# Masks on two row halves, and attention directly ahead of the second step of scores in TensorE's order

## The chip, the cores and the metric

The kernel runs on one core of one Trainium2 chip. The metric is the device time of one execution in microseconds. A core has TensorE (matrix products, PE in the profile, its weight loads PEld), VectorE (DVE), ScalarE (ACT), GpSimd (POOL) and the DMA queue that SyncE issues (SP). Each engine works through its own instructions in a fixed order and waits on the others by semaphores.

## The reference

The input is `x` of 8 sequences x 512 tokens x 128 features. A layer norm without gain gives `xn`, and the result is the sum of three parts.

```python
xn = _layernorm(x)
x = x + attn(xn, ...) + ffn(xn, ...)
```

`attn` is one causal attention with 16 heads of 8 features and relative positions. `ffn` is, in spite of its name, a stack of six layers. Each layer has a local attention and a feed-forward part, both with a residual:

```python
for i in range(DEPTH):                                  # 6
    x = attn_layer(shift_tokens(x), ...) + x            # 16 heads of 64, windows of 32
    x = ffn_layer(shift_tokens(x), ...) + x             # layer norm, 128 -> 2*341, gelu gate, -> 128
```

In `attn_layer`, queries and keys are normalised to unit length per head and rotated. Every window of 32 queries sees its own 32 keys and the 32 keys before it, with this mask:

```python
mask = (it < jb) | (it > jb + w) | (jb == -1)
sim = jnp.where(mask, -jnp.finfo(sim.dtype).max, sim)
attn = jax.nn.softmax(sim, -1)
```

The mask of a query depends on its place in its window only, and, for the first window of a sequence, on the fact that there are no earlier keys.

## The kernel before

The single causal attention (`rel_attention`) runs first, some 500 us. The six local layers (`local_layers`, `steps_of_layers`) fill the rest. Their work is cut into tiles of 128 tokens: 6 layers x 8 sequences x 4 tiles are 192 tiles. The loop over tiles is a hand-written software pipeline. In iteration `n` TensorE works on several tiles at once, and the order of its instructions is exactly the order of the program (`tc.manual_schedule` for TensorE alone). A planner lays out the queues of the other engines at build time by its own estimates of when operands are ready. The order of the steps of one iteration is a string of `ORDERS`, one for each tile position in a sequence: row `n % 4`, called rows 0 to 3 here. The steps are:

- `p0` to `p3` project queries (0, 1) and keys (2, 3) of tile `n + 2`. Each is three products into one PSUM buffer (L641 to L643); VectorE rotates (L771, L772), ScalarE squares (L773), GpSimd adds (L776), VectorE sums the squares (L779 for one part, L781 for the other).
- `r` makes the inverse norms of tile `n + 2` on VectorE (a chain of small operations, L791, L70 to L81), and GpSimd multiplies queries and keys by them (L795). It holds nothing for TensorE.
- `q0 q1 k0 k1` turn queries and keys of tile `n + 1` (L814), and ScalarE copies them out (L817).
- `s0`, `s1` are the two steps of scores of tile `n`. Each fills two PSUM banks. A matmul with an identity first writes the mask into each bank (L836), then 64 matmuls of a 64 x 32 part of the array add the scores (L848). VectorE takes the maxima (L857), and ScalarE makes the exponentials with their sums, eight pairs of instructions (L861). After `s1` the reciprocal of the sums is taken (L873), GpSimd multiplies (L874), and VectorE transposes (`pT`, L876). There are only two such banks (`PSB = (2, 6)`), so the masks of one step wait for the exponentials of the step before.
- `v0` to `v3` make values of tile `n`, already multiplied by the output weights: three products, a copy by ScalarE (L890), and four DMAs on SP's queue (`vw`, L892).
- `a0`, `a1` are attention for tile `n - 1` (`attend`): 64 short matmuls of probabilities and values (L910; 56 for the first tile of a sequence) into one PSUM buffer, then a copy by ScalarE (`ys`, L921).
- `+` adds the result of tile `n - 2` to the state `xt` (a turn at L928, VectorE at L931). After the last tile of a sequence it also starts that sequence's feed-forward part. Each `f` runs one step of that: a split, the mean (L945), the variance (L953), the scaling (L978), three gates and their gelu (L1001), three values, and the output (`f_ps`, L1023), which VectorE adds (L1035).
- `w1`, `w2` make the next layer's value weights on L727 at the first tile of a layer only. Those matmuls work on two row halves: features 0 to 63 into one bank, 64 to 127 into another.

All products but the scores use six PSUM buffers of one pool (`ps_x`) in turn, the inverse norms' scratch (`root_tile`) too.

Of the kernel before, what the change touches and what calls it, by code (L numbers as in the profile page):

```python
# [13 lines left out]
BF16 = mybir.dt.bfloat16  # L14
# [6 lines left out]
P = 128  # L21
# [20 lines left out]
H, D = 16, 64  # L42
# [3 lines left out]


ORDERS = (
    "p0 p1 v0 f s0 w2 + p2 f p3 q0 f f q1 s1 w2 k0 v1 w1 a0 r a1 w1 k1 v2 v3",
    "p0 s0 w2 p1 p2 v0 q0 f p3 f + f q1 s1 w2 k0 v1 w1 a0 r a1 w1 k1 v2 v3 f",  # L50
    "p0 p1 s0 w2 v0 v1 f p2 q0 q1 p3 s1 w2 k0 w1 + a0 r a1 w1 k1 v2 v3",
    "p0 p1 s0 w2 v0 f p2 q0 + q1 p3 v1 s1 w2 k0 w1 a0 r a1 w1 k1 v2 v3",
)
PSB = (2, 6)
VAR = {'Z': '', 'N': '', 'C': '0', 'D': 0, 'hl': 'P', 'xl': 'P', 'fl': 'P', 'v': 'AAAA', 'q': 'AA', 'k': 'AA', 'pr': 'P', 'R5': 0, 'lo2': 'V'}
# [527 lines left out]
def local_layers(tc, i, ident, ident_b, xt, out, spare):  # L583


    with ExitStack() as ctx:
        yield from steps_of_layers(ctx, tc, i, ident, ident_b, xt, out, spare)


def steps_of_layers(ctx, tc, i, ident, ident_b, xt, out, spare):  # L590
    nc = tc.nc

    def pool(name, bufs, **kw):
        return ctx.enter_context(tc.tile_pool(name=name, bufs=bufs, reuse_waits="tile", **kw))
# [13 lines left out]
    def eng(c):  # L608
        return nc.gpsimd if c == "P" else nc.vector
# [4 lines left out]
    def in_turn(step):  # L614


        ins = step.ins
        if "any" in last:
            tc.add_manual_dep(
                ins,  # L620
                last["any"].name,
                mybir.DependencyInfo(mybir.DependencyClass.NoSync, mybir.DependencyReason.DATA),
                reason="one table at a time",
            )
        last["any"] = ins
# [193 lines left out]
    def scores(n, g):  # L819

        t = tiles[n][2]
        if g == 0:
            probs[n] = {
                "pr": p2.tile([P, 2, 2, NW, 2 * W], F32, name="pr"),
                "mx": p2.tile([P, 2, 2, NW], F32, name="mx"),
                "sm": p2.tile([P, 2 * 2 * NW], F32, name="sm"),
            }  # L830
        pr, mx, sm = (probs[n][k] for k in ("pr", "mx", "sm"))
        qT, kT = turned[n]["q"], turned[n]["k"]
        mask = masks[:, 0 if t == 0 else 1].rearrange("p w k -> p (w k)")
        banks = [ps_sc.tile([P, NW, 2 * W], F32, name="sc_ps") for _ in range(2)]
        for ps in banks:
            nc.tensor.matmul(  # L836
                ps.rearrange("p w k -> p (w k)"),
                lhsT=ident_b,
                rhs=mask,
                start=True,  # L840
                stop=False,
                skip_group_check=True,
            )
        for w in range(NW):
            for j in range(4):
                for p, ps in enumerate(banks):
                    r = slice(D * p, D * p + D)
                    nc.tensor.matmul(  # L848
                        ps[32 * j : 32 * j + 32, w, :],
                        lhsT=qT[r, 4 * g + j, W * w : W * w + W],  # L850
                        rhs=kT[r, 4 * g + j, W * w : W * w + 2 * W],
                        start=False,
                        stop=w == NW - 1,
                        skip_group_check=True,
                    )
        for p, ps in enumerate(banks):
            nc.vector.tensor_reduce(mx[:, p, g], ps, AX.X, ALU.max, negate=True)  # L857
            for w in range(NW):
                m = (2 * p + g) * NW + w
                in_turn(  # L860
                    nc.scalar.activation(  # L861
                        pr[:, p, g, w, :],
                        ps[:, w, :],
                        AF.Exp,
                        bias=mx[:, p, g, w : w + 1],
                        accum_out=sm[:, m : m + 1],
                    ),
                )
        if g == 0:
            return  # L870
        del turned[n]
        flat = pr.rearrange("p a g w k -> p (a g w) k")
        nc.vector.reciprocal(sm, sm)  # L873
        eng(VAR["pr"]).tensor_mul(flat, flat, sm.unsqueeze(2).to_broadcast([P, 16, 2 * W]))  # L874
        pT = p2.tile([P, 2, 2, NW, 2, W], F32, name="pT")
        nc.vector.transpose(  # L876
            pT.rearrange("p a g w b q -> p (a g w b q)"), pr.rearrange("p a g w k -> p (a g w k)")
        )
        probs[n] = pT
# [200 lines left out]
    cp = pool("b_const", 1)  # L1080
    p1 = pool("b_p1", 1)
    p2 = pool("b_p2", 2)
    p3 = pool("b_p3", 3)
# [13 lines left out]
    nc.vector.memset(keys[:, :, 0:W], 0.0)  # L1097
    ones = cp.tile([P, P], F32R, name="ones")
    nc.vector.memset(ones.bitcast(F32), 1.0)
    mean_w = cp.tile([P, 1], F32, name="mean_w")  # L1100
    nc.vector.memset(mean_w, 1.0 / E)

    with tc.manual_schedule(engines={nc.tensor.engine}):
        for n in range(-1, len(tiles) + 2):
# [10 lines left out]
            for step in ORDERS[n % NT].split():  # L1115
# [8 lines left out]
                elif kind == "r" and more:  # L1124
                    normalise(n + 2)
                elif kind == "q" and have(n + 1):
                    turn_q(n + 1, k)
                elif kind == "k" and have(n + 1):
                    turn_k(n + 1, k)
                elif kind == "s" and have(n):  # L1130
                    scores(n, k)
                elif kind == "v" and have(n):
                    values(n, k)
                elif kind == "a" and have(n - 1):
                    attend(n - 1, k)
                elif kind == "+" and have(n - 2):
                    add(n - 2)
                    l, b, t = tiles[n - 2]
                    if t == NT - 1:
                        if l not in weights:  # L1140
                            weights[l] = load(l)
                        feeding = feed_forward(l, b, weights[l])
                elif kind == "f":
                    next(feeding, None)
                elif kind == "w":

                    if have(n + k) and tiles[n + k][1:] == (0, 0):
                        next(making, None)
# [95 lines left out]
```

## Time and profile before

| | |
|---|---|
| three runs | 3472.5, 3478.84 (median), 3479.6 us |
| profiled execution | 3475.25 us, span 3473.3 us, granted TensorE clock 0.988 |
| busy share of the span | PE 94%, PEld 69%, DVE 88%, ACT 80%, POOL 80% |
| mask matmuls (L836) | 768, busy 173.5 us, 278 ns each with their pipeline |
| a steady group of four tiles (2089.1 to 2148.5 us) | 59.4 us: PE 57.50 busy, DVE 54.16, ACT 51.13, POOL 51.02 |

Line numbers with an L are lines of the kernel before. In a list of waits, a line names the engine and tile that waited, whom it waited for, the total in us, how often, and the longest. In a chain or timeline, a line begins with its start and its length in us from the start of the span. An instruction's form such as 64*32 gives the rows and columns of the array that it uses. Matmuls are pipelined, so the distance between the starts of two matmuls tells what one costs, not its length.

### The profile page before, as it was taken

Reading aid. Unit: us, or ns where it says so; the run is one execution under the profiler, and the core shown is the slowest. Engines: PE = TensorE matmul, PEld = TensorE weight load, DVE = VectorE, ACT = ScalarE, POOL = GpSimd, SP = SyncE. Lnnn points to the kernel's source line nnn. Section 1 sums busy time; section 2 is a strip of 40 time slices with the busy share of each in tenths; the row PEclk is TensorE's granted clock in tenths of the full one; section 3 lists DMA queues with packets and bytes.
Section 4 is the critical chain, followed back from the end, with each engine's and each line's share of the span. In section 5 each row is a group of like instructions: output and inputs, shape, how many; then the busy total and the mean of one; then the engine's idle time right before and its main releaser. Section 6 shows DMA issues by size and latency. Waiting matters only on the chain.

```text
span 3473.3 us, 130619 instructions
## 1 busy us (share of the span) xinstructions
PE 3253.4 (94%) x50176; PEld 2393.9 (69%) x50176; DVE 3039.7 (88%) x7474; ACT 2791.2 (80%) x9818; POOL 2768.1 (80%) x2130
## 2 busy tenths in 40 slices
PE   6999989999999999899999999998999999999997
PEld 4666657777677777677777677776777776777775
DVE  8788748999899999989998898999989899898994
ACT  3776668888788888788888788888888888888884
POOL 5666668888888888888888788888888888788883
PEclk9999989999999999999999999999999999999998
DMA  1111123232333322333233332323333233233332
GB/s 43 33 33 42 30 64 80 72 74 72 86 82 78 75 72 73 96 77 76 70 75 75 86 84 73 74 72 91 76 77 76 72 74 94 73 83 76 83 76 59
DMA packets 221058, 249.93 MB, mean 72 GB/s; under 512 B 73238, under 2 KB 115604, under 8 KB 220436
## 3 DMA queue, kind: packets, MB, share of 16 engines
q1 hardware_dynamic: 220148, 241.18, 28.2%
q8 instruction: 398, 6.52, 0.8%
q14 instruction: 224, 1.84, 0.2%
q10 hardware_dynamic: 288, 0.39, 0.0%
HBM read 26.92 MB, written 4.19 MB: 9 GB/s over the span
## 4 chain that ended last, share of the span: by engine, by line
PE 44%; DVE 29%; ACT 17%; issue 3%; POOL 3%; DMA 3%; SPq 1%; ACTq 0%; POOLq 0%; DVEq 0%
ACT pr L861 7%; PE y_ps L910 7%; PE qkT_ps L814 6%; DVE q L771 5%; DVE rot L772 5%; PE sc_ps L848 4%; PE f_ps L1023 3%; PE v_ps L641 2%; ACT h L1001 2%; PE v_ps L642 2%; ACT sq L773 2%; DVE pT L876 2%; PE a_o_ps L467 2%; PE v_ps L643 2%; DVE mx L857 2%
## 5 line engine op out<-in xcount | busy, mean ns | idle before, releaser
L861 ACT ACTIVATE pr<-sc_ps,mx 128x64 f32<-128x64 f32 x3072 | 923.1, 347 | 114.8 <-DVE mx L857 110.4
L776 POOL TENSOR_TENSOR q<-q,rot 128x1024 f32<-128x1024 f32 x384 | 934.2, 2433 | 93.1 <-DVE rot L772 58.1
L795 POOL TENSOR_TENSOR q<-q,rn 128x1024 f32<-128x1024 f32 x384 | 725.5, 1910 | 2.1 <-DVE rn L81 1.6
L861 ACT ACTIVATION_READ_ACCUMULATOR pr<-sc_ps,mx 128x1 f32 x3072 | 717.7, 240 | 0.0
L773 ACT ACTIVATE sq<-qk_ps 128x512 f32<-128x512 f32 x768 | 469.8, 632 | 251.7 <-DVE rot L772 158.4
L874 POOL TENSOR_TENSOR pr<-pr,sm 128x1024 f32<-128x1024 f32 x192 | 365.7, 1905 | 340.4 <-DVE rn L81 213.1
L771 DVE TENSOR_TENSOR q<-qk_ps,wrot 128x512 f32<-128x512 f32 x768 | 523.9, 682 | 43.3 <-PE qk_ps L643 38.3
L772 DVE TENSOR_TENSOR rot<-qk_ps,wrot 128x512 f32<-128x512 f32 x768 | 521.4, 679 | 0.0
L890 ACT COPY v<-v_ps 128x512 f32<-128x512 f32 x768 | 469.8, 660 | 52.6 <-PE v_ps L643 24.5
L814 PE MATMUL qkT_ps<-ident,q 128*128 128x128 f32 x3072 | 479.9, 282 | 23.4 <-POOL q L795 14.7
L814 PEld LDWEIGHTS qkT_ps<-ident,q 128*128 128x128 f32 x3072 | 340.2, 141 | 143.8 <-POOL q L795 54.9
L848 PEld LDWEIGHTS sc_ps<-kT,qT 64*32 64x32 f32 x24576 | 272.6, 106 | 180.4 <-issue 178.9
L910 PE MATMUL y_ps<-vw,pT 128*32 128x128 f32 x11904 | 382.5, 275 | 3.6 <-DMA vw<-v 3.4
L910 PEld LDWEIGHTS y_ps<-vw,pT 128*32 128x32 f32 x11904 | 328.1, 110 | 58.1 <-issue 27.3
L641 PE MATMUL qk_ps<-wqk_hi,xs_hi 128*128 128x512 f32 x768 | 349.0, 454 | 19.4 <-ACT ys L921 15.8
L641 PE MATMUL v_ps<-wvo_hi,xs_hi 128*128 128x512 f32 x768 | 339.6, 442 | 11.5 <-ACT ys L921 6.4
L848 PE MATMUL sc_ps<-kT,qT 64*32 64x64 f32 x24576 | 335.6, 226 | 0.7 <-ACT kT L817 0.7
L643 PE MATMUL qk_ps<-wqk_hi,xs_lo 128*128 128x512 f32 x768 | 305.7, 398 | 0.0
L643 PE MATMUL v_ps<-wvo_hi,xs_lo 128*128 128x512 f32 x768 | 304.4, 396 | 0.0
L642 PE MATMUL qk_ps<-wqk_lo,xs_hi 128*128 128x512 f32 x768 | 304.2, 396 | 0.0
L642 PE MATMUL v_ps<-wvo_lo,xs_hi 128*128 128x512 f32 x768 | 303.1, 395 | 0.0
L857 DVE TENSOR_REDUCE mx<-sc_ps 128x4 f32<-128x256 f32 x768 | 282.8, 408 | 11.1 <-PE sc_ps L848 9.5
(201 smaller groups left out, 7198.8 us busy)
## 6 DMA issues: line engine op xcount, KB each, us to landing
vw<-v SPq DMA_DIRECT2D x3072, 64.0 KB
a_qz<-a_qT SPq DMA_DIRECT2D x128, 64.0 KB
wqk_raw<-in_Wqk SPq DMA_DIRECT2D x24, 256.0 KB
wv_raw<-in_WvT SPq DMA_DIRECT2D x12, 256.0 KB
wo_raw<-in_Wo SPq DMA_DIRECT2D x12, 256.0 KB
wrot<-in_trig SPq DMA_DIRECT2D x24, 128.0 KB
a_x<-in_x SPq DMA_DIRECT2D x8, 256.0 KB
a_res<-in_x SPq DMA_DIRECT2D x8, 256.0 KB
```

The source lines that it names most:

```text
L641: nc.tensor.matmul(ps, lhsT=ah, rhs=bh, start=True, stop=False)
L642: nc.tensor.matmul(ps, lhsT=ah, rhs=bl, start=False, stop=False)
L643: nc.tensor.matmul(ps, lhsT=al, rhs=bh, start=False, stop=True)
L771: nc.vector.tensor_mul(q[:, :, a], ps, wide(cos[:, a, :]))
L772: nc.vector.tensor_mul(v[:, :, 1 - a], ps, wide(sin[:, 1 - a, :]))
L773: nc.scalar.activation(sq[:, a], ps, AF.Square)
L776: nc.gpsimd.tensor_add(q, q, v)
L795: nc.gpsimd.tensor_mul(q, q, r[:, m, :].unsqueeze(2).to_broadcast([P, H, D]))
L814: nc.tensor.transpose(tr[:, m, :], q[:, 2 * hp : 2 * hp + 2, :].rearrange("p h d -> p (h d)"), ident)
L848: nc.tensor.matmul(ps[32 * j : 32 * j + 32, w, :], lhsT=qT[r, 4 * g + j, W * w : W * w + W], rhs=kT[r, 4 * g + j, W * w : W * w + 2 * W], ...
L861: nc.scalar.activation(pr[:, p, g, w, :], ps[:, w, :], AF.Exp, bias=mx[:, p, g, w : w + 1], accum_out=sm[:, m : m + 1],),
L910: nc.tensor.matmul(y[W * w : W * w + W, :], lhsT=pT[:, p, g, w, half, :], rhs=v[:, p, g, :], start=(p, g, half) == (0, 0, 0 if keys[w] is ...
```

## The change

The mask of each bank is written from one half of the rows instead of all of them. A new constant `ident_h` holds, in rows 0 to 63 and again in rows 64 to 127, two 64 x 64 identities side by side. With rows 0 to 63 of it as weights and the same rows of the mask as the moving operand, a matmul writes all 128 rows of the first bank; rows 64 to 127 write the second bank. This is the same mask, since it repeats every 32 rows.

In `ORDERS`, `a0 a1` move from behind `s1` and `k0` (in rows 0 and 1 behind `v1` too) to directly ahead of `s1`, in all four rows. `r` stands behind `v1` (rows 0 and 1) or behind `k0` (rows 2 and 3), `v2` moves ahead of `k1`, and `+` moves by one step or a few in rows 0, 1 and 2.

```diff
 ORDERS = (
-    "p0 p1 v0 f s0 w2 + p2 f p3 q0 f f q1 s1 w2 k0 v1 w1 a0 r a1 w1 k1 v2 v3",
-    "p0 s0 w2 p1 p2 v0 q0 f p3 f + f q1 s1 w2 k0 v1 w1 a0 r a1 w1 k1 v2 v3 f",
-    "p0 p1 s0 w2 v0 v1 f p2 q0 q1 p3 s1 w2 k0 w1 + a0 r a1 w1 k1 v2 v3",
-    "p0 p1 s0 w2 v0 f p2 q0 + q1 p3 v1 s1 w2 k0 w1 a0 r a1 w1 k1 v2 v3",
+    "p0 p1 v0 f s0 w2 p2 + f p3 q0 f f q1 a0 a1 s1 w2 k0 v1 r w1 v2 w1 k1 v3",
+    "p0 s0 w2 p1 p2 v0 q0 f p3 f + q1 f a0 a1 s1 w2 k0 v1 r w1 v2 w1 k1 v3 f",
+    "p0 p1 s0 w2 v0 v1 f p2 q0 q1 p3 a0 a1 s1 w2 + k0 w1 r v2 w1 k1 v3",
+    "p0 p1 s0 w2 v0 f p2 q0 + q1 p3 v1 a0 a1 s1 w2 k0 w1 r v2 w1 k1 v3",
 )
@@ scores
-        for ps in banks:
+        for p, ps in enumerate(banks):
+            r = slice(D * p, D * p + D)
             nc.tensor.matmul(
                 ps.rearrange("p w k -> p (w k)"),
-                lhsT=ident_b,
-                rhs=mask,
+                lhsT=ident_h[r].rearrange("r a c -> r (a c)"),
+                rhs=mask[r],
                 start=True,
                 stop=False,
                 skip_group_check=True,
@@ steps_of_layers, constants
+    ident_h = cp.tile([P, 2, P // 2], BF16, name="ident_h")
+    for p in range(2):
+        r = slice(D * p, D * p + D)
+        nc.vector.tensor_copy(ident_h[r], ident[r, r].unsqueeze(1).to_broadcast([D, 2, D]))
```

## The prediction

> **What bounds the kernel now.** I read the page's busy shares and the shares of the chain that ended last, then the waits, then the chain itself over one steady group of four tiles (2089 to 2149 us), then timelines inside that group. The page first:
>
> ```profile
> span 3473.3 us, 130619 instructions
> ...
> PE 3253.4 (94%) x50176; PEld 2393.9 (69%) x50176; DVE 3039.7 (88%) x7474; ACT 2791.2 (80%) x9818; POOL 2768.1 (80%) x2130
> ...
> PE 44%; DVE 29%; ACT 17%; issue 3%; POOL 3%; DMA 3%; SPq 1%; ACTq 0%; POOLq 0%; DVEq 0%
> ```
>
> No engine is the bound alone: TensorE is busiest, but it holds only 44% of the chain, and VectorE, ScalarE and GpSimd hand work to each other with little room. The waits that the change can touch:
>
> ```profile
> PE sc_ps L836 <- ACT pr L861: 80.2, 142, 1.4
> PEld qkT_ps L814 <- POOL q L795: 54.9, 93, 2.4
> ```
>
> The first is TensorE at a mask matmul whose score bank is still being read by the exponentials of the step before. The second is the turning of queries or keys, waiting for GpSimd's normalising multiply. The chain over one group shows where the first counts (start, length, what):
>
> ```profile
> 2094.61 1.69 ACT pr L861 x11
> ...
> 2096.34 0.27 PE sc_ps L836
> ...
> 2116.21 0.39 ACT pr L861 x3
> ...
> 2116.68 0.61 ACT v L890
> ...
> 2117.33 0.50 PE mean_ps L945
> ...
> 2124.58 0.83 ACT pr L861 x5
> ...
> 2125.46 0.27 PE sc_ps L836
> ...
> 2130.72 0.25 DVE sm L873
> ```
>
> The chain enters TensorE at the second scores step (`s1`) of the ORDERS-row-0 tile, because the exponentials of `s0` ended late; it stays on TensorE through row 1 (but for ScalarE's copy before the mean), enters at `s1` of row 2 in the same way, and goes to VectorE at the reciprocal that follows row 2's second exponentials. Row 3 is VectorE's, the start of row 0 ScalarE's.
>
> **The waits, term one.** In this group's timeline the idle time before masks is 0.23 and 0.91 us in row 0, 0.11 in row 2 and 0.39 in row 3: 1.64 us, times 48 groups 79 us, which agrees with the 80.2 of the waits. Attention takes about 2.0 us of TensorE (1.95 to 2.06 in the timeline), more than any of these, so directly ahead of `s1` it covers all of them. Row 3's part (0.39 x 48 = 19 us) lies where the chain is on VectorE and buys nothing. Row 0's and row 2's are on the chain: 1.25 x 48 = 60 us.
>
> How much of the 60 stays is decided at the next join, row 1's first turn of queries:
>
> ```profile
> 2102.70 1.90 POOL L874 TENSOR_TENSOR pr<-pr,sm 128x1024 f32<-128x1024 f32 x1 [4.04 <-DVE rn L81]
> 2104.56 3.76 POOL L795 TENSOR_TENSOR q<-q,rn 128x1024 f32<-128x1024 f32 x2
> ...
> 2106.17 0.39 PE L643 MATMUL v_ps<-wvo_hi,xs_lo 128*128 128x512 f32 x1
> 2106.52 0.66 PE L814 MATMUL qkT_ps<-ident,q 128*128 128x128 f32 x4
> ```
>
> GpSimd ends the first multiply at 2104.56 + 1.91 = 2106.47 and TensorE turns at 2106.52. Without that wait TensorE would have followed its last matmul by 0.23, at 2106.40: the two paths tie within 0.12 us. GpSimd's path (second exponentials, reciprocal, L874, L795) does not begin with TensorE: row 0's maxima waited 2 us behind the L781 sum on VectorE, which waited for ScalarE. So if GpSimd keeps L874 ahead of L795, row 0's gain ends at this turn, and 0.12 of its 1.14 us stays. If the planner puts L795 first (its input was ready at 2102.66, L874's at 2102.61, and after the change the second exponentials come later in the program's time), the turn is free 1.9 us earlier and all of it stays. The queues of GpSimd, VectorE and ScalarE are laid out by the planner anew and the trace cannot show which: bounds 0 and 60 us, and I take the middle, 30.
>
> **The masks, term two.** Two full masks cost little:
>
> ```profile
> 2103.09 0.39 PE L836 MATMUL sc_ps<-masks,ident_b 128*128 128x256 bf16 x2
> 2103.41 0.86 PE L848 MATMUL sc_ps<-kT,qT 64*32 64x64 f32 x64
> ...
> 1467.48 1.16 PE L727 MATMUL wvo_ps<-wo_raw,wv_raw 64*128 64x128 f32 x16
> 1468.57 0.64 PE L910 MATMUL y_ps<-vw,pT 128*32 128x128 f32 x16
> ```
>
> From the first mask to the first score are 0.32 us. A mask that had waited alone starts 0.20 before the scores (2096.34 to 2096.54), so one mask streams in 0.12 and the passage into the scores' shape (64*32) adds 0.08 to 0.09. The halved masks have the shape of L727 (64*128), the only row of the trace with row halves: 16 matmuls in 1.09 us, the passage out included, 0.068 each, against 0.12 for a full 128-column turn (four from 2106.52, the next group at 2107.01). So two halves run beside each other in about the time of one: 0.11 saved per pair. The passage in and out is the counter-item: at `s0` the mask follows a same-shaped projection today and will follow across a change of shape, about 0.09 lost of the 0.11. At `s1` attention (128*32) stands directly ahead: its exit and the mask's entry are one passage, so all 0.11 stays. Per tile 0.13 us, times 192 = 25 us of TensorE work; by TensorE's 44% of the chain, 11 us. Bounds: 0 (a halved mask is held by its weight load; the loads stay 768, and L836's, 98 ns, are hidden now) and 25.
>
> The Trainium skill's page "TensorEngine Tiling (Array Packing)", section Tiling Modes, says that changing the tiling mode drains the array. It speaks against this change, and the 0.08 to 0.09 us above are what this trace shows of it; without a drain, "halved masks cost half", term two would be 192 x 0.22 = 42 us of work and 18 on the chain, and the sum 3431.
>
> **Other edits, one answer each.** `ident_h` is one tile and two 64x128 VectorE copies, some 0.6 us once by the 0.28 us of the 64x128 add at L931, before the first scores at 506 us, while VectorE has room: 0, at most 0.6. `v2` ahead of `k1` changes no TensorE total; its four DMA issues on SP's queue go 0.5 us earlier, and their readers come more than 5 us later. `+` past `p2` or `q1`, and in row 2 ahead of `k0`: a 0.11 us turn and two 0.28 us adds, no reader within a microsecond but row 1's feed-forward, whose first step moved with it: 0. `r` issues nothing on TensorE; it orders VectorE and GpSimd, and that is in term one. Attention itself issues no DMA; its `vw` rows and its transposed probabilities must be there 2 us sooner. In this group's timeline the transposes end 4.9, 3.8, 2.2 and 4.4 us before the new places in rows 1, 2, 3 and 0: covered, unless L874 falls behind both L795 (3.8 us), where row 3 would wait 1.6.
>
> **Sum.** Against the profiled execution (3475.25 us; span 3473.3 and 2 around it): 3475.25 - 30 - 11 = 3434. The median of the three runs, 3478.84, is 3.6 above the profiled one: **3438**.
>
> **Rivals.** (1) *Tie at row 1's turn*: L874 stays first, 0.12 + 0.11 of the 1.25 us stay (11 us), masks 11, and up to 0.4 us a group goes back at row 3's turn, which stands behind L795 too (0.10 us idle before it in this group): 3457 to 3476. For it: the tie above. Against: attention's output copy and key copies now come at other times, so the planner's queues will not be the same. (2) *Slower: attention no longer covers the second exponentials.* Today attention, which needs one PSUM buffer for 2 us, stands between `s1` and `k1 v2 v3`, while ScalarE works 2.4 us on exponentials and copies nothing out. Afterwards `k0 v1 v2 k1 v3` and row 1's mean, each wanting one of six buffers, come in those 2 us. Its place is the mean's wait of the chain above (ScalarE's copy at 2116.68, the mean at 2117.33), and row 2's reciprocal, where VectorE takes over. `s1` itself is up to 2.0 us later where it had no wait (row 1) and 1.9 in row 2, VectorE's maxima absorb 0.2 to 1.9 of that. Price 0.3 to 1.0 us a group, 14 to 48 us; with row 0's gain lost and masks of 11 gained, 3482 to 3516. It decides once the second exponentials end over 0.3 us later than now. (3) *The change does not halve the masks* (the pair runs one after the other, with the passages): 2 passages a tile, 0.1 x 192 x 0.44 = 8 us lost instead of 11 gained; 3457 if the rest holds.
>
> **How the numbers follow.** Forecast, rival 3 in it: 0.48, own range 3407 (60 + 11 gained) to 3464 (15 gained). Rival 1: 0.15; rival 2: 0.37. No change is what a measurement here cannot tell, 0.2%: 3472 to 3486. Faster: 0.48 and 0.06 of rival 1 is 0.54; same: 0.09 of rival 1 and 0.02 of rival 2, 0.11; slower 0.35, the rest of rival 2, with the case of row 3 waiting for probabilities in it. Range 3402 to 3520: it leaves out about 0.08 below and 0.1 above.
>
> **What would show it.** Right: the wait at the masks falls from 80 us to under 30; the two masks of a pair start within 20 ns; attention is followed by the masks without idle time; GpSimd runs L795 ahead of L874 in row 0. Rival 1: TensorE's wait for L795 rises from 55 to over 90 us. Rival 2: idle time before the mean, the projections or `s0`'s masks, ended by ScalarE's copies or exponentials. The forecast is wrong if VectorE's share of the chain, not TensorE's, takes up what the waits gave.

## The result and the profile after

The changed kernel takes 3853.53 us (median of four runs, 3846.57 to 3856.83), against 3479.22 us for the kernel before in runs beside it: a ratio of 1.1077, 95% interval 1.1058 to 1.1096. It is 374 us slower, where 41 faster was forecast, and it lies outside the range. All times below are of fast executions, so a single slow one of `behind_k1` (8864 us) and one of `five_buffers` (4146 us at a granted clock of 0.70, the one that was profiled) are left out. In the profile of the changed kernel all lines from L837 on are one higher than before (masks L837, scores L849, exponentials L862, value copies L891, the `vw` DMAs L893, attention L911, its copy `ys` L922). The page, the three lines that answer to those of before:

```profile
span 3844.6 us, 130866 instructions
...
PE 3410.4 (89%) x50176; PEld 2471.6 (64%) x50176; DVE 3059.6 (80%) x7476; ACT 2804.6 (73%) x9818; POOL 2769.7 (72%) x2130
...
PE 18%; ACT 12%; DVE 5%; DMA 4%; SPq 4%; issue 1%; POOL 0%; POOLq 0%; ACTq 0%; DVEq 0%
```

VectorE, ScalarE and GpSimd do nearly the same work as before (20, 13 and 2 us more) in a span that is 371 us longer, so each of them idles 350 to 370 us longer. DMA and SP's queue, 4% of the chain before, are 8 of the 44 points that the chain still accounts for. What TensorE waits for, in its own list of waits:

```profile
PE val_ps L641 <- ACT qT L817: 124.2, 40, 3.1
PE y_ps L911 <- DMA vw<-v: 63.0, 195, 2.1
PE wvo_ps L727 <- DMA wo_raw<-in_Wo: 48.1, 6, 10.2
PE y_ps L911 <- DVE pT L877: 26.6, 44, 3.2
PE y_ps L911 <- ACT v L891: 17.0, 24, 1.5
...
PE y_ps L911 <- ACT sq L773: 12.6, 9, 2.5
...
PE sc_ps L837 <- ACT pr L862: 0.3, 1, 0.3
```

The wait at the masks (80.2 us) is gone: 0.3 us of it are left. In its place stand 124 us in row 0, where a feed-forward product waits for ScalarE's copy of turned queries to free a buffer, some 129 us at attention (the four lines shown and small ones; 3.4 before), and 48 us at the next layer's value weights, whose DMAs are issued on SP's queue, as those of `vw` are. The same list for ScalarE, first before, then after:

```profile
ACT pr L861 <- DVE mx L857: 110.4, 149, 3.0
...
ACT qT L817 <- PE qkT_ps L814: 27.8, 42, 2.0
...
ACT ys L921 <- PE y_ps L910: 6.4, 3, 5.5
...
ACT kT L817 <- PE qkT_ps L814: 2.0, 5, 0.9
```

```profile
ACT ys L922 <- PE y_ps L911: 254.8, 181, 5.7
ACT pr L862 <- DVE mx L858: 154.4, 132, 3.7
ACT kT L817 <- PE qkT_ps L814: 126.7, 93, 2.4
ACT qT L817 <- PE qkT_ps L814: 104.6, 84, 3.2
```

They sum to 147 us before and 641 after. In three of the four, what ScalarE wants next comes from attention itself (`ys`) or from a step that now stands behind attention in TensorE's order (the second scores for `mx`, the keys for `kT`). The turned queries (`qT`) stand ahead of attention; in row 0 they come late because TensorE itself has waited. One row 0 shows how it happens. Timeline of the changed kernel, TensorE and then ScalarE (start, length, engine, line, what; in brackets the idle time before and what ended it):

```profile
2293.69 0.46 PE L641 MATMUL val_ps<-fx_hi,w_hi 128*85 128x512 f32 x1 [3.10 <-ACT qT L817]
...
2295.42 3.12 PE L911 MATMUL y_ps<-vw,pT 128*32 128x128 f32 x64
2298.48 0.28 PE L837 MATMUL sc_ps<-masks,ident_h 64*128 64x256 bf16 x2
2298.69 0.86 PE L849 MATMUL sc_ps<-kT,qT 64*32 64x64 f32 x64
```

```profile
2295.53 0.59 ACT L817 COPY qT<-qkT_ps 128x512 f32<-128x512 f32 x1 [1.39 <-PE qkT_ps L814]
2296.01 0.60 ACT L773 ACTIVATE sq<-qk_ps 128x512 f32<-128x512 f32 x1
2298.70 0.27 ACT L922 COPY ys<-y_ps 128x128 f32<-128x128 f32 x1 [2.08 <-PE y_ps L911]
2300.17 0.59 ACT L817 COPY kT<-qkT_ps 128x512 f32<-128x512 f32 x1 [1.21 <-PE qkT_ps L814]
2300.66 0.32 ACT L862 ACTIVATE pr<-sc_ps,mx 128x64 f32<-128x64 f32 x1
```

First TensorE stands for 3.1 us until ScalarE has worked off the first exponentials and a copy. Then TensorE spends 3.1 us on attention, and ScalarE, with nothing left to copy, stands: 1.39, 2.08 and 1.21 us around it. The two take turns. In the kernel before, the same stretch of row 0 (TensorE's line, then ScalarE's):

```profile
2098.61 1.95 PE L910 MATMUL y_ps<-vw,pT 128*32 128x128 f32 x64
```

```profile
2098.06 0.66 ACT L817 COPY kT<-qkT_ps 128x512 f32<-128x512 f32 x1
2098.76 0.59 ACT L890 COPY v<-v_ps 128x512 f32<-128x512 f32 x1
2099.86 0.31 ACT L861 ACTIVATE pr<-sc_ps,mx 128x64 f32<-128x64 f32 x1 [0.51 <-DVE mx L857]
```

While TensorE is in attention, ScalarE copies keys and values and begins the second exponentials, VectorE takes their maxima, and ScalarE's only pause is 0.51 us. That work was there because `s1`, `k0` and `v1` stood ahead of attention. A steady tile takes 17.25 us after, by the starts of the first masks over 176 tiles, and 15.31 before; ScalarE is busy 13.0 us of it after and 12.9 before. (Some expectations below give a tile of the new order 16 or 16.4 us; it is 17.25 in the changed kernel.)

The long wait has a second cost. The stretches of that row 0 in the changed kernel (from:to, length, busy times, then the granted clock):

```profile
2292.00:2295.00 3.00, 1.31 (x6) 1.06 (x7) 1.69 (x4) 2.14 (x10) 2.61 (x2) 0.91 0.09 22
2295.00:2299.00 4.00, 4.00 (x102) 3.17 (x101) 2.69 (x5) 1.35 (x3) 0.24 (x1) 0.64 0.01 4
2299.00:2303.00 4.00, 4.00 (x73) 3.34 (x51) 2.23 (x10) 2.83 (x18) 0.82 (x1) 1.00 0.00 0
```

After the 3.1 us of idle the clock falls. It averages 0.64 over the four microseconds of the second line; in the trace's clock record it is 0.50 for 3.41 us, from 2294.45 us on, 0.76 us after TensorE has taken up work again. Attention takes 3.12 us here instead of 1.95. The changed kernel has 56 stretches at half clock in all, the kernel before 17. Over the span the mean granted clock is 0.965 against 0.988, which is (1 - 0.965) x 3844.6 - (1 - 0.988) x 3473.3 = 93 us of full clock at most. The Trainium skill, "TensorE: Matmul & The Clock Gate", Part 1, says that an idle window of about 3.4 us brings the clock to half and about 3.4 us of sustained work bring it back. The half and the length of the slow stretch agree with this trace; the idle time ahead of it, 3.10 us, is a little shorter than the page's window.

### The profile page after: what moved, and what is told of

Read it like the earlier page. It is cut to its first block, busy times and chain, and to the rows that moved or that the text cites. A ratio compares the mean times of both kernels' runs of the same rounds, so it can differ in the third digit from the quotient of the medians.

```text
span 3844.6 us, 130866 instructions
## 1 busy us (share of the span) xinstructions
PE 3410.4 (89%) x50176; PEld 2471.6 (64%) x50176; DVE 3059.6 (80%) x7476; ACT 2804.6 (73%) x9818; POOL 2769.7 (72%) x2130
## 5 line engine op out<-in xcount | busy, mean ns | idle before, releaser
L795 POOL TENSOR_TENSOR q<-q,rn 128x1024 f32<-128x1024 f32 x384 | 724.0, 1907 | 531.2 <-DVE rn L81 531.2
L862 ACT ACTIVATE pr<-sc_ps,mx 128x64 f32<-128x64 f32 x3072 | 921.7, 342 | 155.3 <-DVE mx L858 154.4
L862 ACT ACTIVATION_READ_ACCUMULATOR pr<-sc_ps,mx 128x1 f32 x3072 | 707.8, 234 | 0.0
L911 PE MATMUL y_ps<-vw,pT 128*32 128x128 f32 x11904 | 543.6, 300 | 136.1 <-DMA vw<-v 63.0
L911 PEld LDWEIGHTS y_ps<-vw,pT 128*32 128x32 f32 x11904 | 409.6, 120 | 276.5 <-issue 84.8
L773 ACT ACTIVATE sq<-qk_ps 128x512 f32<-128x512 f32 x768 | 492.7, 650 | 115.7 <-DVE rot L772 74.4
L891 ACT COPY v<-v_ps 128x512 f32<-128x512 f32 x768 | 474.6, 649 | 44.7 <-DMA vw<-v 31.7
L814 PE MATMUL qkT_ps<-ident,q 128*128 128x128 f32 x3072 | 470.4, 279 | 8.1 <-POOL q L795 5.7
L814 PEld LDWEIGHTS qkT_ps<-ident,q 128*128 128x128 f32 x3072 | 368.0, 142 | 96.2 <-POOL q L795 10.2
L641 PE MATMUL v_ps<-wvo_hi,xs_hi 128*128 128x512 f32 x768 | 353.5, 460 | 13.1 <-DVE xt L932 11.2
L849 PE MATMUL sc_ps<-kT,qT 64*32 64x64 f32 x24576 | 334.2, 225 | 7.7 <-issue 6.8
L817 ACT COPY kT<-qkT_ps 128x512 f32<-128x512 f32 x384 | 242.8, 633 | 126.7 <-PE qkT_ps L814 126.7
L849 PEld LDWEIGHTS sc_ps<-kT,qT 64*32 64x32 f32 x24576 | 270.0, 106 | 57.0 <-issue 11.1
```

Source lines behind the costliest of these rows:

```text
L641: nc.tensor.matmul(ps, lhsT=ah, rhs=bh, start=True, stop=False)
L773: nc.scalar.activation(sq[:, a], ps, AF.Square)
L795: nc.gpsimd.tensor_mul(q, q, r[:, m, :].unsqueeze(2).to_broadcast([P, H, D]))
L814: nc.tensor.transpose(tr[:, m, :], q[:, 2 * hp : 2 * hp + 2, :].rearrange("p h d -> p (h d)"), ident)
L849: nc.tensor.matmul(ps[32 * j : 32 * j + 32, w, :], lhsT=qT[r, 4 * g + j, W * w : W * w + W], rhs=kT[r, 4 * g + j, W * w : W * w + 2 * W], ...
L862: nc.scalar.activation(pr[:, p, g, w, :], ps[:, w, :], AF.Exp, bias=mx[:, p, g, w : w + 1], accum_out=sm[:, m : m + 1],),
```

## The experiments

Times over the kernel before are differences to the median of its runs beside them, 3474 to 3479 us. The letters are those of the texts on record: in the first four, A is a loop through the freshness of attention's inputs, B the moved `+`, C the changes of array shape; from `fixed_values` on, C is the missing cover for ScalarE.

**The parts.** Full masks stay where nothing is said of halves.

```diff
 halves_only:  halved masks, ORDERS of before
 orders_only:  full masks, ORDERS of after
 attend_only:  full masks, only attention moved, as in row 0:
-    "... f f q1 s1 w2 k0 v1 w1 a0 r a1 w1 k1 v2 v3",
+    "... f f q1 a0 a1 s1 w2 k0 v1 w1 r w1 k1 v2 v3",
 rest_only:    full masks, ORDERS of after, but attention back behind k0 or v1, around r
```

> The order of before with the masks on two row halves. Theory A (the place of attention closes a loop over the values' copies and DMAs) and rival B (the moves of + and v2, which let the feed-forward's third value product wait for a buffer that ScalarE empties late) both expect no harm: a pair of masks takes 0.2 instead of 0.3 us, so 3455 to 3480 us. Rival C (the change of array shape at the masks is what costs, about 0.5 us at each of 384 steps) expects over 3600 us.

> The order of after with the full masks of before. A and B expect 3850 to 3890 us, the changed kernel's time plus some 0.1 us a mask pair. C expects near 3480.

> Full masks; of the new order only this: a0 a1 directly ahead of s1; +, f, v2 and k1 stand as before. A expects most of the loss, over 3700 us, and TensorE waiting at y_ps for the vw DMAs. B expects little of it: 3480 to 3560, since + stands ahead of p2 and the third value product finds its buffer.

> Full masks; the new order with a0 and a1 put back around r behind k0 or v1: +, f and v2 ahead of k1 stay moved. A expects 3460 to 3520 us. B expects the wait at val_ps of some 1.8 us in every tile of row 0 and half or more of the loss, over 3620 us.

Measured: `halves_only` 1.000 (0.999 to 1.001), `orders_only` 1.111 (1.1085 to 1.1135), `attend_only` 1.1113 (1.1082 to 1.1143), `rest_only` 1.002 (1.0009 to 1.0031). Of the edits, the place of attention alone makes the loss. B falls with `attend_only`, which leaves `+` where it was; array shapes fall with `halves_only`. In `attend_only` row 0 waits in the same way, only one step further on:

```profile
PE qkT_ps L814 <- ACT qT L817: 88.8, 37, 2.4
PE y_ps L910 <- DMA vw<-v: 54.2, 177, 2.2
```

**Older inputs, first try.** `two_back` lets attention work on the tile before (with one more buffer each for probabilities and values, and the closing addition one tile later, not shown here), `early_values` moves the value steps ahead of attention.

```diff
 two_back
-                elif kind == "a" and have(n - 1):
-                    attend(n - 1, k)
+                elif kind == "a" and have(n - 2):
+                    attend(n - 2, k)
 early_values (row 0)
-    "p0 p1 v0 f s0 w2 p2 + f p3 q0 f f q1 a0 a1 s1 w2 k0 v1 r w1 v2 w1 k1 v3",
+    "p0 p1 v0 f s0 w2 v1 p2 + f v2 p3 q0 f v3 f q1 a0 a1 s1 w2 k0 r w1 w1 k1",
```

> The changed kernel with attention in the same new place of TensorE's order, but on the tile before the last (and the closing addition one tile later), so that its vw rows and its transposed probabilities are a whole period (some 15 us) older. Theory A (the place is harmless, the inputs are too fresh: values copied after the second exponentials, four to twelve DMA issues of 0.6 us on SP's queue, 2 to 4 us of landing, then attention, which now stands ahead of the next second scores, so that the loop closes in 16 us): TensorE's waits for vw<-v (67.7 + 63.0 us) and for pT (26.6) fall below 10 us, time 3420 to 3500. Rival R (the place itself: two microseconds of attention no longer stand between the second scores and the keys and values that want PSUM buffers, and row 0 waits for the qT copy's buffer): the waits for the qT copy (141.5 + 124.2 us) stay above 60, time above 3700.

> The changed kernel with the projections of the values (v1, v2, v3) moved ahead of attention and the second scores, so that their copies and DMAs do not wait for the second exponentials; attention's place and tile are as in the changed kernel. Theory A (the loop goes through the values' copies and DMAs): TensorE's waits for vw<-v fall from 131 us to under 30, time 3460 to 3600. Rival P (the loop goes through the probabilities: GpSimd's multiply that writes them stands behind the multiply by rn, so the transposes are late): the wait for pT rises from 27 to over 60 us, time above 3700. Rival R (the place itself): waits for the qT copy stay above 60 us each, time above 3700.

Both missed by far: 1.2585 (1.2564 to 1.2606) and 1.2065 (1.2045 to 1.2085). The waits for `vw` are gone, as A wanted, and others stand there. TensorE's in `two_back`, then in `early_values`:

```profile
PE rstd_ps L979 <- POOL dg L972: 317.3, 96, 7.1
PE qkT_ps L814 <- POOL q L795: 288.4, 47, 8.6
```

```profile
PE qkT_ps L814 <- POOL q L795: 323.1, 137, 4.0
```

Neither wait is large in the changed kernel. Each new order also lets the planner lay out the queues of GpSimd, VectorE and ScalarE anew, and `two_back` shifts the feed-forward by a row besides. The mean granted clock falls too, to 0.891 and 0.934, which by the sum above is at most 435 of the 899 us that `two_back` loses and 235 of the 719 of `early_values`. Neither kernel tests A by itself. They are the reason to hold the queues in what follows; what the new queues cost in these two was not measured.

**Queues held.** The queues of one kernel are imposed on another by an edge, without a wait, from each instruction to the one ahead of it in the wanted order (the core of the edit; the rest looks up that order).

```diff
+            tc.add_manual_dep(
+                x,
+                after[x.engine],
+                mybir.DependencyInfo(mybir.DependencyClass.NoSync, mybir.DependencyReason.DATA),
```

> Full masks and the changed ORDERS, so TensorE's order is exactly that of orders_only (1.111 of the time before), but every other engine's queue (ScalarE, VectorE, GpSimd, SP) is pinned, instruction for instruction, to the order that it has in the kernel before; without the pins the planner lays them out anew. Theory A (the place in TensorE's order closes the loop second scores, exponentials, value copies, DMA, attention): the loop is there whatever the queues, 3650 to 3900. Theory Q (the place is not the cost: the planner's new queues are, above all VectorE's, where the inverse norms and the transposes of probabilities now stand behind other tiles' work): 3440 to 3560.

> The mirror: full masks and the ORDERS of before, so TensorE's order is exactly that of before, but ScalarE's, VectorE's, GpSimd's and SP's queues are pinned to the order that they have in orders_only. Theory A: the loop is open again, 3480 to 3600. Theory Q: the queues bring their cost with them, 3700 to 3900.

> Full masks, the changed ORDERS, VectorE's and GpSimd's queues pinned to their order in the kernel before, ScalarE's and SP's laid out by the planner (it puts ys, then the second exponentials, then k0, v1, v2, k1, v3). In place_old_queues ScalarE's pinned order, with k0 and v1 ahead of the second exponentials, did not fit the place; here it does. If VectorE's and GpSimd's new order was the cost (theory Q), 3480 to 3600. If the place is (theories A and C), 3750 to 3900.

Measured: the new place with all old queues 1.0927 (1.0906 to 1.0948); the old place with all new queues 1.1075 (1.1056 to 1.1093); the new place with VectorE's and GpSimd's old queues 1.088 (1.0864 to 1.0896). Q falls as the sole cause, since the place costs 321 us with all old queues and 307 with VectorE's and GpSimd's. The slower clock is not needed either: with all old queues it is 0.988, as before. But A fails the mirror: TensorE's order is that of before and the whole loss is there. ScalarE's waits say why (in these kernels, lines of the local layers are two higher than before, and in `fixed_values` three from attention on). The old place with the new queues, then the new place with the old queues:

```profile
ACT ys L923 <- PE y_ps L912: 448.9, 190, 5.6
```

```profile
ACT kT L819 <- PE qkT_ps L816: 335.4, 175, 3.8
```

In the mirror ScalarE's queue has `ys` ahead of the second exponentials, so ScalarE waits out attention although the scores are there. In the other, its queue has the copy of `k0` next, and `k0` comes behind attention. Either order alone leaves ScalarE waiting during attention.

**The loop through the values.** `fixed_values` is `orders_only` with its own queues held and one operand exchanged: attention reads a fixed tile of zeros. The values are still made and moved, but they are left out of the result.

```diff
+                    v = fixed
                     nc.tensor.matmul(
                         y[W * w : W * w + W, :],
                         lhsT=pT[:, p, g, w, half, :],
                         rhs=v[:, p, g, :],
```

> orders_only with all queues pinned to its own order, but attention's products read a fixed tile of zeros in place of the vw rows; the values, their copies and their DMAs are all still made, nobody waits for them. This takes one arc out of the loop and leaves every engine's queue as it is. Theory A (the loop through the value copies and DMAs sets the 16.4 us of a tile): TensorE's waits for vw<-v (about 120 us) are gone and the time is 3480 to 3620. Theory C (ScalarE's queue sets it: the output copy ys now stands ahead of the second exponentials, so ScalarE idles during attention, and TensorE's buffers come free late): the waits for the qT copy in row 0 (140 us) stay, 3750 to 3860.

Measured: 3815.9 us, 1.0977 (1.0958 to 1.0997), 44 us less than the 3859.6 of `orders_only`. So A's loop is real and worth some 44 us. Added up over the timeline from its first to its last matmul, attention takes 386 us before, 594 in `orders_only` and 422 here: most of what late values stretch it by goes, and TensorE waits elsewhere for most of that time. The rest stays, in C's range:

```profile
PE val_ps L643 <- ACT qT L819: 126.8, 41, 3.1
...
PE mean_ps L948 <- DVE rn L83: 35.5, 36, 2.3
PE y_ps L913 <- DVE pT L878: 30.7, 46, 3.2
```

The wait in row 0 is untouched, and the transposed probabilities hold attention for 31 us.

**Row by row, by halves, and one exchange.** Old orders except as shown, the planner free. The single rows move attention alone, as `attend_only` does, and not `+` or `v2`, as two of the expectations say.

```diff
 row0_only ... row3_only: halved masks, only attention moved, in that row alone
 half_ahead (row 0; all rows alike)
-    "... f f q1 s1 w2 k0 v1 w1 a0 r a1 w1 k1 v2 v3",
+    "... f f q1 a0 s1 w2 k0 v1 w1 r a1 w1 k1 v2 v3",
 behind_s1 (against orders_only, all rows)
-    "... f f q1 a0 a1 s1 w2 k0 v1 r w1 v2 w1 k1 v3",
+    "... f f q1 s1 a0 a1 w2 k0 v1 r w1 v2 w1 k1 v3",
```

> Halved masks, the old orders in rows 1 to 3, and only row 0's attention moved directly ahead of its second scores (with row 0's other moves). Theory A: one row in four has no 16 us period to close a loop with, since rows 1 to 3 give the time back; time 3450 to 3500, the wait at the second scores' masks falls by 60 us. Rival R, by which each moved row costs on its own: a quarter of the 374 us or more, 3550 to 3600 (row 0 holds the wait for the qT copy, so up to 3650).

> Halved masks, the old orders in rows 0, 2 and 3, and only row 1's attention moved directly ahead of its second scores (with row 1's other moves). Row 1's second scores waited for nothing before. Theory A: 3475 to 3520, since attention finds row 0's last vw DMA under way and waits 0 to 1.5 us for it. Rival R: 3530 to 3600.

> Halved masks, attention moved ahead of the second scores in row 2 alone. Rows 0 and 1 alone cost 60 and 63 us. If rows add up (theory C, each row pays for its own missing cover), rows 2 and 3 hold the other 250: 3560 to 3620. If the loss needs all four rows (a loop that closes only when no row gives time back), 3480 to 3540.

> The same for row 3 alone. If rows add up: 3560 to 3640. If the loss needs all four rows: 3470 to 3540. Row 3 has no feed-forward step between its second scores and the next first scores but two steps of them behind those.

> The kernel before with only a0, half of attention's products, directly ahead of the second scores; a1 and everything else stay. Theory C: one of the two microseconds of cover is gone and one buffer is held across the second scores, so between a third and two thirds of the loss: 3570 to 3730. Theories A and P: the loops close by 1 us less, under a third of it, 3480 to 3570.

> orders_only with one exchange: attention directly behind the second scores instead of directly ahead of them (s1 a0 a1 k0 v1 ...), all else as in the changed ORDERS. Theory C (cover: ScalarE's second exponentials, with the copies queued behind them, are late for TensorE's six buffers unless attention's two microseconds and one buffer stand between the second scores and the next keys and values): 3460 to 3530. Theories A and P (inputs too fresh: vw rows or transposed probabilities): attention is only 1 us later than in orders_only, so most of the loss stays, 3700 or more.

| kernel | ratio (95%) | over before, us | ScalarE's four waits, us |
|---|---|---|---|
| before | | 0 | 147 |
| `row0_only` | 1.0171 (1.0154 to 1.0187) | 60 | 217 |
| `row1_only` | 1.0183 (1.0167 to 1.0198) | 63 | 221 |
| `row2_only` | 1.012 (1.0102 to 1.0138) | 45 | 250 |
| `row3_only` | 1.0276 (1.0261 to 1.0292) | 97 | 218 |
| `half_ahead` | 1.0537 (1.0518 to 1.0556) | 187 | 375 |
| `orders_only` | 1.111 (1.1085 to 1.1135) | 383 | 660 |
| `behind_s1` | 1.0224 (1.0208 to 1.024) | 78 | 217 |
| `place_old_dve` | 1.088 (1.0864 to 1.0896) | 307 | 451 |
| `place_old_queues` | 1.0927 (1.0906 to 1.0948) | 321 | 501 |
| `fixed_values` | 1.0977 (1.0958 to 1.0997) | 339 | 628 |
| `old_place_new_queues` | 1.1075 (1.1056 to 1.1093) | 376 | 669 |

The last column sums ScalarE's waits for `ys`, `kT` and `qT` on TensorE and for the maxima on VectorE. It rises with the large losses; among the single rows and `behind_s1` it does not order them. The exchange of attention and second scores gives back 305 of 383 us, which a loop through the values, worth 44, cannot; `half_ahead` costs half. Both are as C expects, `behind_s1` 22 us above its range. One row alone costs 45 to 97 us, so each pays by itself. Of the two ranges in the expectations, rows 1 and 3 land in that of rows that add up, row 2 in that of a loss that needs all four, and row 0 between them. The four add up to 264 of the 374 us. The other 110 appear only together; the 44 of the loop and the 93 of the clock may be part of them, but they were not split further. What a row pays is seen in row 0 alone (TensorE's list):

```profile
PE y_ps L911 <- ACT sq L773: 83.8, 47, 2.0
...
PE sc_ps L837 <- ACT pr L862: 24.9, 60, 1.4
```

The wait at the masks falls by 55 us, and attention, which has taken its place, waits 84 us for a buffer. The mask had to wait for the exponentials; attention's buffer waits for what ScalarE does after them.

**The other side, and the buffers.**

```diff
 behind_k1 (row 0; all rows alike)
-    "... f f q1 s1 w2 k0 v1 w1 a0 r a1 w1 k1 v2 v3",
+    "... f f q1 s1 w2 k0 v1 w1 r k1 a0 a1 w1 v2 v3",
 five_buffers
-PSB = (2, 6)
+PSB = (2, 5)
```

> The kernel before with attention one step later: behind k1 instead of between k0 (or v1) and k1, in all rows. Attention directly ahead of the second scores cost 386 us, directly behind them 78, at its old place 0. If later cover and older inputs are still better, 3440 to 3470; if the old place is the best one, since three buffers are then asked for before attention gives ScalarE its time, 3480 to 3560. I expect the second.

> The kernel before with five shared PSUM buffers for TensorE's products instead of six, nothing else. Theory C says that TensorE is held to ScalarE by these buffers and that the kernel before stands close to that limit: with one fewer, TensorE waits in the same places as in the changed kernel (val_ps for the qT copy, y_ps for sq, v_ps for ys), 3650 to 3950. If the buffers have room to spare, 3475 to 3540.

Measured: `behind_k1` 1.1077 (1.1057 to 1.1098), far above what was expected, and `five_buffers` 1.0919 (1.0894 to 1.0945), a time that C expects; where its waits stand is not shown. One buffer is worth 321 us, and TensorE's six have no room. In `behind_k1` ScalarE's four waits sum to 148 us, as before; its lists of waits, TensorE's and ScalarE's, name others:

```profile
PE qkT_ps L814 <- ACT sq L773: 115.8, 129, 2.4
PE sc_ps L836 <- ACT pr L861: 66.9, 91, 1.3
```

```profile
ACT sq L773 <- DVE rot L772: 398.9, 276, 5.5
```

ScalarE waits 399 us for VectorE's rotations (158 before), and TensorE for ScalarE's squares. Whether that is the place or VectorE's new queue was not tried, so this side stays open. No kernel of the study beats the kernel before.

## Why the prediction was wrong

**The waits (term one).** Every sign named for it came true: the wait at the masks is gone, attention is followed by the masks without idle time, GpSimd runs L795 ahead of L874 (in 177 of 184 steady tiles, in all rows), VectorE's share of the chain did not rise (29% before, 5% of a chain that accounts for only 44%). And the time went the other way. The step that failed is the account behind "Attention takes about 2.0 us of TensorE, more than any of these, so directly ahead of `s1` it covers all of them". It books what the step covers at its new place and not what it uncovers at its old one. At the old place the second scores, the keys and in two rows a value step stood ahead of attention, and ScalarE and VectorE worked on them meanwhile; at the new place ScalarE stands and TensorE then waits for its buffers. The old cover is attention's length: 192 tiles x 1.95 us are 374 us for the move, half of it 187 for `half_ahead`. Measured are 374 (383 with full masks) and 187. That agreement is in part luck. The waits at the masks should come off, and the clock and the value loop go on top; by the same count each row alone would cost 94 us, and 45 to 97 were measured; and `behind_k1` loses 376 us without these waits of ScalarE. The length gives the size at best; `behind_s1` and the kernels with held queues give the cause.

**The second rival named the mechanism and was mis-sized.** "Attention no longer covers the second exponentials", with six buffers as the way in which it reaches TensorE, was the right rival. Its price, "0.3 to 1.0 us a group", was read from two joins of one group. Measured are 374 / 48 = 7.8 us a group, four times attention's length. Its range of 3482 to 3516 should have reached what the length and the number of tiles give, 374 us, as the waits of term one were worked out over all groups.

**Edits costed at nothing.** "covered" was said of attention's inputs after the transposes alone had been looked at, and only in their old places. In the changed kernel attention waits 26.6 us for `pT` and 63.0 for the `vw` rows, whose DMAs were never priced; `fixed_values` puts the loop through the values at 44 us. The other moves, `v2`, `+` and `r`, cost 0.2% (0.09 to 0.31%) together: nothing to speak of, as forecast. The wait for attention's own buffer was in no term, and it is 84 us in `row0_only`.

**The masks (term two).** The work is saved as predicted: the two masks of a pair start 3 ns apart (median; 121 before), and the scores follow the first by 0.21 us, not 0.32.

```profile
2303.30 0.28 PE L837 MATMUL sc_ps<-masks,ident_h 64*128 64x256 bf16 x2
2303.52 0.86 PE L849 MATMUL sc_ps<-kT,qT 64*32 64x64 f32 x64
```

In time it stays open. `halves_only` changes nothing (0, with 3.5 us on either side), but it keeps the old order, where both pairs of a tile follow a change of shape. By the prediction's own count that saves 0.02 us a pair and 3.4 us on the chain, which this interval cannot tell from nothing. At the new place the changed kernel stands against `orders_only`: 1.1077 against 1.111, some 9 to 11 us for the halved masks, near the 11 of the forecast, but the two intervals overlap. The third rival, a pair that runs one after the other, falls with the 3 ns.

**The first rival** (a tie at row 1's turn) did not happen: the weight loads' wait for L795 fell from 54.9 to 10.2 us instead of rising.

## What to carry to other kernels

A long step on one engine that gives nothing to the others until it ends should stand behind steps that have just given them work. Before pricing the wait that it fills at a new place, price what it covers at the old one: its length there, times the number of tiles, is an estimate of what can be lost (374 us in this case, where the whole move measured 374; for one row alone it gives 94, and 45 to 97 were measured). For a moved step look at everything that it waits for: operands, their DMAs, and the buffer that it writes. Where a planner lays out the other queues, an order moved on one engine changes them too, so hold the queues in an experiment before its time is read as the price of the move.

## What the runs showed of the hardware

In the changed kernel a wait of 3.1 us on TensorE was followed, 0.76 us after work began again, by 3.41 us at half the granted clock, and the attention in them took 3.12 us instead of 1.95. Two mask matmuls on different row halves started 3 ns apart (median), two full ones 121 ns apart. One DMA issue of value rows holds SP's queue for some 0.6 us in the chain, and each tile makes sixteen of them:

```profile
2310.08 0.59 SPq L893
2310.72 0.59 SPq L893
2311.35 2.03 DMA vw<-v
```

The two issues start 0.64 us apart, so sixteen would take some 10 us of a tile's 17 (an estimate), and here attention goes on only after the landing, 3.3 us after the first of them.
